# LSTM and a three-layer sign network: Wx's transfers in another order, two fewer steps of x Wx ahead of the recurrence

## The chip, the cores and the metric

The kernel runs on one core of one Trainium2 chip. The metric is the device time of that core in microseconds, the median of the runs shown. The profile is one further execution, taken by the hardware profiler; its own time stands beside its span below.

## The reference

An LSTM runs over 64 steps for 32 sequences, its hidden states go through three dense layers whose weights are +1 or −1, and the result is added to x.

```python
# x: (32, 64, 256), cond_1024: (32, 256) is h0, Wx and Wh: (256, 1024), b: (1024,)
xW = jnp.einsum('ntd,dg->ntg', x, Wx) + b
def step(carry, xw_t):
    prev_h, prev_c = carry
    a = xw_t + prev_h @ Wh
    i = jax.nn.sigmoid(a[:, :Hd])
    f = jax.nn.sigmoid(a[:, Hd:2 * Hd])
    o = jax.nn.sigmoid(a[:, 2 * Hd:3 * Hd])
    g = jnp.tanh(a[:, 3 * Hd:])
    next_c = f * prev_c + i * g
    next_h = o * jnp.tanh(next_c)
    return ((next_h, next_c), next_h)

# k0: (512, 1024), k1: (1024, 1024), k2: (1024, 256), booleans: True is 1, False is -1
h = jnp.concatenate([hs, -hs], axis=-1)
h = s0 * dense(k0, h)
h = jax.nn.relu(h) * 2
h = s1 * dense(k1, h)
h = jax.nn.relu(h) * 2
h = s2 * dense(k2, h)
return x + h
```

## The kernel before

**Layout.** 256 hidden units are four quarters (q) of 64. A time step's gates lie on 128 partitions, a quarter's 32 sequences on each 32 of them, and four gates of 64 columns side by side. A product for a time step is therefore cut into four column strips of TensorE (4 × 32), for two halves k of the contraction. Gates stand in slots in the order 3, 0, 1, 2 (`GATES`), so slots 1, 2 and 3 are neighbours in Wx as well. In the trace an fp32 product is two instructions.

**Before the loop.** VectorE clears `warm` and `idle`; TensorE runs two products of zeros into the gate banks and eight (`WARM_UP`) into `p_idle` (L643 to L646), while x's first eight steps and Wx come in over two DMA queues, that of SyncE (SP) and that of ScalarE (ACT). `load_gates` (L121) issues one transfer for a group of slots and a range of k; given two engines it cuts the 128 rows into halves. Loads on these two queues take turns on eight semaphores, so that a ninth load is issued after the landing of an earlier one. VectorE turns x (`turn_x`, L229), and TensorE forms x Wx for the first eight steps in four PSUM banks: k = 0 for slots 1 and 2, then k = 0 for slots 0 and 3, then `copy_bias` (L657; 16 small products and a copy by VectorE), then k = 1 for all slots, with an eviction by VectorE that adds the bias (`evict_x`, L261) after every second step. `x_products` (L275) then goes on up to time step `AHEAD`.

**The loop over 64 steps.** Each step has the gates' products from h (`gates_from_h`, L304), then `cell_step` (L322): sigmoid and tanh on ScalarE, products on VectorE, tanh(c), h, a transposition of h into `hist`, and two ScalarE copies of the next step's x part into the gate banks (L319, L320). TensorE fills the time of that chain with other work, in passes that a generator yields:

```python
goal = (t + 1) * total_x // X_STEPS if t < X_STEPS else (t + 1 - X_STEPS) * total_ffn // (T - X_STEPS)
while done < goal:
    left_over[0] = goal - done
    done += next(work)
```

In the first `X_STEPS` steps the passes are x Wx of the time steps from `AHEAD` on, four to a time step (L249; a pass is four products with two slots, or half of four with four slots). In the others they are the FFN of the blocks 0 to 2 of 16 time steps each (`ffn_block`, L588). Block 3 follows after the loop in `last_block`, another algorithm.

**The FFN's passes.** A block has 192 passes of one 128 × 512 product each: 32 in the first layer (L594), 128 in the second (L620), 32 in the third (L607). An accumulation that ends is taken by `evict` (L365): ScalarE's relu makes a high part (L368), VectorE the low part (L369), and the next layer multiplies both. The third layer goes along two accumulations behind the second; at the end of a block, after the second layer's last accumulation m = 7, the order is:

```python
yield from layer2([(0, last - 2), (0, last - 1), (1, last - 2)])
yield from layer2([(0, last), (1, last - 1), (1, last)])
outputs.append(output(b, po))
```

Each pair is two passes, one for the high and one for the low part. `output` is then taken step by step (VectorE's transpositions, the addition of x, the stores). The order on every engine is the order in which the program emits instructions: a step's evictions stand behind its `cell_step`. Conversions of the weights' bits (`make_w0`, `make_w1`, `make_w2`), splits of h into two parts (`split_h`) and sums for the last block are dealt out at the ends of steps.

Of the kernel before, what the change touches and what calls it, by code (L numbers as in the profile page):

```python
# [43 lines left out]
def lstm_ffn(ctx: ExitStack, tc: tile.TileContext, x, cond, wx_d, wh_d, b_d, k0_d, k1_d, k2_d, s0_d, s1_d, s2_d, out):  # L44
    nc = tc.nc
    P = 128
# [10 lines left out]
    TB = SB * N  # L57
# [1 line left out]

    GATES = (3, 0, 1, 2)  # L60

    AHEAD = 12
    X_STEPS = 21

    FIRST_CHORE = 2
    W2_STEP = 24
# [4 lines left out]
    const = ctx.enter_context(tc.tile_pool(name="const", bufs=1))  # L71
# [12 lines left out]
    def act(shape, dtype, name):  # L84
        return apool.tile(shape, dtype, tag="act", name=name)
# [5 lines left out]
    def load_x(i, half, engines, part=slice(0, SB // 2)):  # L91
        if part.start == 0:
            xq[i, half] = xpool.tile([P, SB // 2, HQ], F32, tag="x", name=f"x{i}_{half}")
        t0 = i * SB + half * (SB // 2)
        for q in range(NQ):
            engines[q % len(engines)].dma_start(  # L96
                out=xq[i, half][q * N : (q + 1) * N, part],
                in_=x[:, t0 + part.start : t0 + part.stop, ts(q, HQ)],
            )
# [5 lines left out]
    wx = wpool.tile([P, 2, G], F32, tag="wx", name="wx")  # L105
# [2 lines left out]
    w2 = const.tile([P, 2, FC1, P], F32R, name="w2")  # L108

    warm = const.tile([P, 40], F32, name="warm")  # L110
    nc.vector.memset(warm, 0.0)
    idle = const.tile([P, 512], mybir.dt.bfloat16, name="idle")
    nc.vector.memset(idle, 0.0)

    first = warm[:, 4 : 4 + N]
    nc.vector.memset(first[:1], 1.0)
# [4 lines left out]
    def load_gates(t, w_d, slots, engines, chunks=slice(0, 2)):  # L121

        w_rows = w_d.rearrange("(p b) g -> p b g", b=2)
        s0, n, g0 = slots[0], len(slots), GATES[slots[0]]
        if len(engines) == 1:
            halves = [slice(0, P)]
        else:
            halves = [slice(0, P // 2), slice(P // 2, P)]
        for engine, half in zip(engines, halves):
            engine.dma_start(  # L130
                out=t[half, chunks, s0 * H : (s0 + n) * H], in_=w_rows[half, chunks, g0 * H : (g0 + n) * H]
            )


    both = [nc.sync, nc.scalar]
    load_x(0, 0, both)
    for k in range(2):
        load_gates(wx, wx_d, (1, 2), [nc.sync], slice(k, k + 1))
        for slot in (0, 3):
            load_gates(wx, wx_d, (slot,), [nc.scalar], slice(k, k + 1))  # L140
    load_x(0, 1, both)
    load_gates(wh, wh_d, (1, 2), both)
    load_gates(wh, wh_d, (0,), [nc.scalar])
# [19 lines left out]
    for i in range(2):  # L163
        t = act([P, 2, F0], U8, f"k0_{i}")
# [64 lines left out]
    def turn_x(i, half, part=slice(0, SB // 2)):  # L229
        if part.start == 0:  # L230
            xT[i, half] = act([P, SB // 2, 2, N], F32, f"xT{i}_{half}")
        nc.vector.transpose(  # L232
            xT[i, half][:, part], xq[i, half][:, part].rearrange("p t (j b) -> p t b j", b=2)
        )
# [10 lines left out]
    def x_part(p, t, k, slots, start):  # L245

        i, s = divmod(t, SB // 2)
        for q in range(NQ):
            nc.tensor.matmul(  # L249
                p[q * N : (q + 1) * N, t % 2, slots],  # L250
                xT[i // 2, i % 2][:, s, k, :],
                wx_q[:, k, q, slots],
                start=start,
                stop=False,
                skip_group_check=True,
            )
# [4 lines left out]
    def evict_x(p, t):  # L261
        xg[t] = gpool.tile([P, 2, 4 * HQ], F32, tag="xg", name=f"xg{t}")
        b = bias.rearrange("p g j -> p (g j)").unsqueeze(1).to_broadcast([P, 2, 4 * HQ])
        load[0] += 1
        nc.vector.tensor_tensor(xg[t], p.rearrange("p t g j -> p t (g j)"), b, ALU.add)  # L265

    def next_x(half):

        if half < 2 * NB:
            load[0] += 1  # L270
            turn_x(*divmod(half, 2))
            if half + 4 < 2 * NB:
                load_x(*divmod(half + 4, 2), [nc.sync])

    def x_products(t0, t1):  # L275

        for t in range(t0, t1, 2):
            p = x_bank(t)
            for s in range(2):
                for k in range(2):  # L280
                    start = s == 0 and k == 0
                    passes = min(left_over[0], 2)
                    if passes == 1:
                        x_part(p, t + s, k, slice(0, 2), start)
                        yield 1
                        x_part(p, t + s, k, slice(2, 4), False)
                    else:
                        x_part(p, t + s, k, slice(0, 4), start)
                    if s == 1 and k == 1:
                        evict_x(p, t)  # L290
                        half, left = divmod(t + 2, SB // 2)
                        if left == 2 and half + 1 < 2 * NB:
                            turns.append(half + 1)
                        if left == 6 and turns:
                            next_x(turns.popleft())
                    yield passes
# [50 lines left out]
    def split_h(i):  # L347

        b, s = divmod(i, SB // SH)
        if s == 0:  # L350
            hparts[b] = (
                hpool.tile([P, 2, TB], F32R, tag="hhi", name=f"hhi{b}"),
                hpool.tile([P, 2, TB], F32R, tag="hlo", name=f"hlo{b}"),
            )
        hi, lo = (p[:, :, ts(s, SH * N)] for p in hparts[b])
        full = hist.pop(i)
        if b == NB - 1:

            hi, lo = (a.rearrange("p k (n t) -> p k t n", n=N) for a in (hi, lo))
            full = full.rearrange("p k (t n) -> p k t n", n=N)  # L360
        nc.scalar.copy(hi, full)
        nc.vector.tensor_tensor(lo, full, hi, ALU.subtract)
# [277 lines left out]
    outputs = deque()  # L640

    p_idle = ps_f.tile([P, TB], F32, tag="pf", name="p_idle")
    for g in gate_banks:  # L643
        nc.tensor.matmul(g, idle[:, :P], idle, start=True, stop=True)
    for n in range(WARM_UP):
        nc.tensor.matmul(p_idle, idle[:, :P], idle, start=True, stop=True)  # L646
    turn_x(0, 0, slice(0, SB // 4))
    turn_x(0, 0, slice(SB // 4, SB // 2))
    for i in range(4):
# [7 lines left out]
    def copy_bias():  # L657
        p_bias = ps_o.tile([P, 4, HQ], F32, tag="po", name="p_bias")
        for q in range(NQ):
            for i, t in enumerate(b_row):  # L660
                nc.tensor.matmul(  # L661
                    p_bias[q * N : (q + 1) * N, 2 * i : 2 * i + 2],
                    first,
                    t.rearrange("p g (q j) -> p q g j", q=NQ)[:, q],
                    start=(i == 0),
                    stop=True,
                    skip_group_check=True,
                )
        nc.vector.tensor_copy(bias, p_bias)

    banks = [x_bank(t) for t in range(0, SB // 2, 2)]
    for slots in (slice(1, 3), slice(0, 4, 3)):
        for t in range(SB // 2):
            x_part(banks[t // 2], t, 0, slots, t % 2 == 0 and slots.start == 1)
    copy_bias()
    for t in range(SB // 2):
        x_part(banks[t // 2], t, 1, slice(0, 4), False)
        if t % 2:
            evict_x(banks[t // 2], t - 1)
            if t == 1:  # L680
                turn_x(0, 1)
    nc.vector.transpose(hT, h_first.rearrange("p (j b) -> p b j", b=2))
    for _ in x_products(SB // 2, AHEAD):
        pass
# [3 lines left out]
    def ffn():  # L688
        for b in range(NB - 1):
            yield from ffn_block(b)  # L690
        yield from last_block(NB - 1)
# [8 lines left out]

    work = x_products(AHEAD, T)
    total_x = (T - AHEAD) * 4
    total_ffn = (NB - 1) * (4 * FC0 + 2 * FC0 * FC1 + 4 * FC1)
    done = 0
    for t in range(T):
# [5 lines left out]
        if outputs:  # L711
            load[0] += 1
            if next(outputs[0], "end") == "end":
                outputs.popleft()
        if t == X_STEPS:
            work, done = ffn(), 0
# [4 lines that stand above are left out]
        if t == X_STEPS - 1:  # L721
            next(work, None)

        if turns and load[0] < 2:
            next_x(turns.popleft())
        if splits and (load[0] < 2 or t >= X_STEPS or t == SH * splits[0] + 2 * SH - 1):
            split_h(splits.popleft())
        else:
# [4 lines left out]
            elif t >= W2_STEP and chores2:  # L733
                chores2.popleft()()
            if w0_parts and (load[0] < 2 or t == X_STEPS - 1):
                w0_parts.popleft()()
# [34 lines left out]
```

## Time and profile before

| | |
|---|---|
| median of 3 runs | 312.17 us (311.9 to 312.34) |
| profiled execution | 312.77 us, span 311.0 us |
| TensorE busy | 304.9 us, 98% |
| VectorE, ScalarE busy | 177.6 us, 143.1 us |
| first gates / first FFN step / last step | 17.4 / 80.8 / 260.0 us |
| moved by DMA | 10.88 MB |

In the rows of the profile PE is TensorE's products, PEld its weight loads, DVE is VectorE, ACT ScalarE, SP SyncE; L249 is line 249 of the kernel. A row of a timeline gives start, duration, engine, line, operation, out<-in, and in brackets the idle time before it and what ended it. Products are pipelined: a row's duration reaches beyond the start of the next, and the time that a product costs is read from start to start. A row of waits gives the total, the number of times and the longest. The span runs from the first instruction to the last; the profiled execution's time has 1.8 us around it.

### The profile page before, as it was taken

What the parts mean: (1) busy time and instruction counts of PE and PEld (TensorE: products, weight loads), DVE (VectorE), ACT (ScalarE), POOL (GpSimd) and SP (SyncE); (2) the same over time, 40 slices, a digit from 0 to 9 for tenths busy, and PEclk for the clock granted to TensorE, in tenths of its full rate; (3) what the DMA queues carried; (4) which work ended last, traced back from release to release, by engine and by line L of the source; (5) the groups of instructions that cost most, each with busy time, mean ns of one, the idle gap of its engine ahead of it and who ended that gap; (6) DMA issues with size and microseconds to landing.
All of it is one profiled execution on the core that took longest, in us unless ns stands there. A gap on an engine that the chain in (4) does not pass through costs nothing.

```text
span 311.0 us, 9795 instructions
## 1 busy us (share of the span) xinstructions
PE 304.9 (98%) x4138; PEld 242.4 (78%) x4138; DVE 177.6 (57%) x527; ACT 143.1 (46%) x512; POOL 6.6 (2%) x24
## 2 busy tenths in 40 slices
PE   7999999999999999999999999999999999999994
PEld 3888888787777777777777777777777777899994
DVE  2466767777673444455755444568564444599441
ACT  0224657774564543444633433356443333786320
POOL 5300000000000000000000000000000000000000
PEclk9999999999999999999999999999999999999999
DMA  6864001143000000000010000000410000031001
GB/s 186 210 185 108 6 10 49 36 93 67 3 2 0 2 2 0 3 2 0 2 38 14 22 1 2 2 2 6 98 34 2 3 0 2 25 80 32 2 0 68
DMA packets 27450, 10.88 MB, mean 35 GB/s; under 512 B 23560, under 2 KB 26632, under 8 KB 27408
## 3 DMA queue, kind: packets, MB, share of 16 engines
q1 hardware_dynamic: 24768, 8.66, 11.3%
q10 hardware_dynamic: 2400, 1.57, 1.8%
q8 instruction: 32, 0.52, 0.7%
q14 instruction: 10, 0.08, 0.1%
q0 software_dynamic: 240, 0.04, 0.1%
HBM read 8.16 MB, written 2.10 MB: 33 GB/s over the span
## 4 chain that ended last, share of the span: by engine, by line
PE 96%; DMA 1%; DVE 1%; SPq 0%; ACT 0%; issue 0%; ACTq 0%
PE p L620 30%; PE gates L308 20%; PE px L249 18%; PE p L594 8%; PE po L607 7%; PE gates L459 4%; PE r L459 2%; PE x L459 2%; PE po L564 2%; PE p L486 2%; DMA wx<-in_L_cond_Wx_dram 1%; SPq L96 0%; DVE a_7l L369 0%; DVE o L574 0%; PE p_bias L661 0%
## 5 line engine op out<-in xcount | busy, mean ns | idle before, releaser
L308 PEld LDWEIGHTS gates<-wh,hist 128*32 128x32 f32 x2016 | 54.6, 109 | 22.3 <-issue 13.4
L308 PE MATMUL gates<-wh,hist 128*32 128x192 f32 x2016 | 68.1, 275 | 0.0
L249 PE MATMUL px<-wx,xT 128*32 128x256 f32 (+1 forms) x1168 | 60.7, 355 | 0.4 <-DMA wx<-in_L_cond_Wx_dram 0.4
L325 ACT ACTIVATE sig<-gates 128x128 f32<-128x128 f32 x64 | 17.7, 277 | 79.8 <-PE gates L308 79.6
L249 PEld LDWEIGHTS px<-wx,xT 128*32 128x32 f32 x1168 | 42.2, 111 | 12.3 <-DVE xT L232 1.3
L329 DVE TENSOR_TENSOR kept<-sig,c 128x64 f32<-128x64 f32 x63 | 14.2, 225 | 49.1 <-ACT sig L325 48.8
L335 ACT ACTIVATE th<-c 128x64 f32<-128x64 f32 x64 | 16.4, 257 | 31.4 <-DVE c L333 31.4
L337 DVE TENSOR_TENSOR h<-sig,th 128x64 f32<-128x64 f32 x64 | 14.4, 225 | 20.7 <-ACT th L335 20.7
L265 DVE TENSOR_TENSOR xg<-px,bias 128x512 f32<-128x512 f32 x32 | 21.2, 670 | 2.8 <-PE px L249 2.3
L319 ACT COPY gates<-xg 128x192 f32<-128x192 f32 x64 | 20.0, 313 | 1.5 <-DVE xg L265 1.5
L594 PE MATMUL p<-hhi,w 128*128 128x512 f32 x48 | 19.3, 402 | 0.0
L594 PE MATMUL p<-hlo,w 128*128 128x512 f32 x48 | 19.1, 397 | 0.0
L342 DVE STREAM_TRANSPOSE hist<-h 128x64 f32<-128x64 f32 x64 | 15.7, 245 | 2.4
L333 DVE TENSOR_TENSOR c<-kept,new 128x64 f32<-128x64 f32 x64 | 14.4, 225 | 2.2
L327 ACT ACTIVATE sig<-gates 128x64 f32<-128x64 f32 x64 | 14.9, 233 | 0.1
L326 ACT ACTIVATE cand<-gates 128x64 f32<-128x64 f32 x64 | 14.0, 218 | 0.0
L331 DVE TENSOR_TENSOR new<-sig,cand 128x64 f32<-128x64 f32 x64 | 13.9, 217 | 0.0
L320 ACT COPY gates<-xg 128x64 f32<-128x64 f32 x64 | 13.0, 203 | 0.0
L594 PEld LDWEIGHTS p<-hhi,w 128*128 128x128 f32 x48 | 9.0, 188 | 2.1
L594 PEld LDWEIGHTS p<-hlo,w 128*128 128x128 f32 x48 | 9.0, 188 | 1.9
L214 ACT ACTIVATE w<-bits,nsgn,sgn 128x1024 fp32r<-128x1024 uint8 x8 | 9.9, 1240 | 0.0
L620 PE MATMUL p<-a_7h,w 128*128 128x512 f32 x24 | 9.9, 412 | 0.0
(250 smaller groups left out, 603.1 us busy)
## 6 DMA issues: line engine op xcount, KB each, us to landing
x<-in_x_dram SPq DMA_DIRECT2D x52, 64.0 KB, 2.7
out_dram<-o SPq DMA_DIRECT2D x28, 64.0 KB, 1.8
bits<-in_L_ffn_k_dram SPq DMA_DIRECT2D x10, 128.0 KB, 2.7
wx<-in_L_cond_Wx_dram SPq DMA_DIRECT2D x2, 256.0 KB, 4.8
wx<-in_L_cond_Wx_dram ACTq DMA_DIRECT2D x4, 128.0 KB, 5.1
wh<-in_L_cond_Wh_dram ACTq DMA_DIRECT2D x2, 256.0 KB, 5.3
wh<-in_L_cond_Wh_dram SPq DMA_DIRECT2D x2, 256.0 KB, 5.8
k<-in_L_ffn_k_dram SPq DMA_DIRECT2D x2, 256.0 KB, 3.1
```

What stands on the lines that cost most here:

```text
L249: nc.tensor.matmul(p[q * N : (q + 1) * N, t % 2, slots], xT[i // 2, i % 2][:, s, k, :], wx_q[:, k, q, slots], start=start, stop=False, ski ...
L265: nc.vector.tensor_tensor(xg[t], p.rearrange("p t g j -> p t (g j)"), b, ALU.add)
L308: nc.tensor.matmul(g[q * N : (q + 1) * N], hT[:, k, :], wh_q[:, k, q, slots], start=False, stop=(k == 1), skip_group_check=True,)
L319: nc.scalar.copy(gates[0], x_t[:, :3])
L325: nc.scalar.activation(sig[:, 0:2, :], gates[0][:, 1:3], AF.Sigmoid)
L327: nc.scalar.activation(sig[:, 2, :], gates[1][:, 0], AF.Sigmoid)
L335: nc.scalar.activation(th, c, AF.Tanh)
L342: nc.vector.transpose(hT, h.rearrange("p (j b) -> p b j", b=2))
L459: nc.tensor.matmul(bank[pair][:, i], a(k)[:, ts(2 * pair + i, P)], b(k, n), start=first and i == 0 and k == 0 and n == 0, stop=last and k ...
L594: nc.tensor.matmul(p, w0[:, k, ts(m, P)], a[:, k, :], start=(n == 0), stop=(n == 3))
L607: nc.tensor.matmul(po[m], w2[:, m, k], a1[k][n], start=(k == 0 and n == 0), stop=(k == FC1 - 1 and n == 1))
L620: nc.tensor.matmul(p1[m], w1[:, k, ts(m, P)], a0[k][n], start=(k == 0 and n == 0), stop=(k == FC0 - 1 and n == 1),)
```

## The change

`AHEAD` goes from 12 to 10 and `X_STEPS` from 21 to 22, so 54 time steps of x Wx are dealt over 22 steps of the loop in place of 52 over 21, and the FFN's 576 passes over 42 in place of 43. `idle` shrinks from 512 columns to 128, is cleared ahead of `warm`, and is read four times over as the moving operand of the same ten zero products. Wx's six transfers become: slots 1 and 2 of k = 0 by halves of the rows on both queues, slot 3 on SP, slot 0 on ACT, then slots 1 to 3 of k = 1 on SP as one piece of 384 KB, and slot 0 of k = 1 on ACT. `copy_bias` moves from ahead of k = 1 to behind its second time step.

```diff
-    AHEAD = 12
-    X_STEPS = 21
+    AHEAD = 10
+    X_STEPS = 22
...
     warm = const.tile([P, 40], F32, name="warm")
+    idle = const.tile([P, P], mybir.dt.bfloat16, name="idle")
+    nc.vector.memset(idle, 0.0)
     nc.vector.memset(warm, 0.0)
-    idle = const.tile([P, 512], mybir.dt.bfloat16, name="idle")
-    nc.vector.memset(idle, 0.0)
...
     load_x(0, 0, both)
-    for k in range(2):
-        load_gates(wx, wx_d, (1, 2), [nc.sync], slice(k, k + 1))
-        for slot in (0, 3):
-            load_gates(wx, wx_d, (slot,), [nc.scalar], slice(k, k + 1))
+    load_gates(wx, wx_d, (1, 2), both, slice(0, 1))
+    load_gates(wx, wx_d, (3,), [nc.sync], slice(0, 1))
+    load_gates(wx, wx_d, (0,), [nc.scalar], slice(0, 1))
+    load_gates(wx, wx_d, (1, 2, 3), [nc.sync], slice(1, 2))
+    load_gates(wx, wx_d, (0,), [nc.scalar], slice(1, 2))
     load_x(0, 1, both)
...
     p_idle = ps_f.tile([P, TB], F32, tag="pf", name="p_idle")
+    zeros = idle.unsqueeze(1).to_broadcast([P, TB // P, P])
     for g in gate_banks:
-        nc.tensor.matmul(g, idle[:, :P], idle, start=True, stop=True)
+        nc.tensor.matmul(g, idle, zeros, start=True, stop=True)
     for n in range(WARM_UP):
-        nc.tensor.matmul(p_idle, idle[:, :P], idle, start=True, stop=True)
+        nc.tensor.matmul(p_idle, idle, zeros, start=True, stop=True)
...
-    copy_bias()
     for t in range(SB // 2):
         x_part(banks[t // 2], t, 1, slice(0, 4), False)
+        if t == 1:
+            copy_bias()
         if t % 2:
             evict_x(banks[t // 2], t - 1)
```

## The prediction

> **What bounds the kernel now.** I read the page first (busy shares, chain), then the timeline of TensorE at the start, at step boundaries of both halves of the loop and at the last step, then who waited for whom.
>
> The page:
>
> ```profile
> span 311.0 us, 9795 instructions
> PE 304.9 (98%) x4138; PEld 242.4 (78%) x4138; DVE 177.6 (57%) x527; ACT 143.1 (46%) x512; POOL 6.6 (2%) x24
> PE 96%; DMA 1%; DVE 1%; SPq 0%; ACT 0%; issue 0%; ACTq 0%
> ```
>
> TensorE is nearly always busy and is 96% of the chain that ended last. So the change can only matter where TensorE idles, switches or waits, and in how often it does so. The start, in the timeline of TensorE:
>
> ```profile
> 1.24 1.04 PE L644 MATMUL gates<-idle 128*128 128x512 bf16 x2 [1.24 <-DVE idle L113]
> 6.11 4.16 PE L249 MATMUL px<-wx,xT 128*32 128x128 f32 x128 [0.42 <-DMA wx<-in_L_cond_Wx_dram]
> 17.42 1.08 PE L308 MATMUL gates<-wh,hT_first 128*32 128x192 f32 x31
> ```
>
> After the zero products there is one hole, 0.42 us, put down to Wx; from 6.11 us on there is none before the first step at 17.42. Step boundaries, two stretches of the same view:
>
> ```profile
> 44.59 1.08 PE L308 MATMUL gates<-wh,hist 128*32 128x192 f32 x32
> 47.63 1.08 PE L308 MATMUL gates<-wh,hist 128*32 128x192 f32 x32
> 50.51 1.08 PE L308 MATMUL gates<-wh,hist 128*32 128x192 f32 x32
> 80.82 1.08 PE L308 MATMUL gates<-wh,hist 128*32 128x192 f32 x32
> 85.01 1.08 PE L308 MATMUL gates<-wh,hist 128*32 128x192 f32 x32
> 89.19 1.08 PE L308 MATMUL gates<-wh,hist 128*32 128x192 f32 x32
> ```
>
> A step with ten passes of x Wx takes 3.04 us (47.63 − 44.59), one with nine 2.88. A step with thirteen FFN passes takes 4.18. Who waited, TensorE's loads:
>
> ```profile
> PEld gates L308 <- issue: 13.4, 38, 0.4
> PEld po L607 <- DVE a_7l L369: 0.5, 1, 0.5
> ```
>
> The first row is the switch from FFN weights back to gate weights, about 0.35 us at 38 of the 43 FFN steps. The second is a real wait, once, in the last step, in the timeline:
>
> ```profile
> 260.01 1.08 PE L308 MATMUL gates<-wh,hist 128*32 128x192 f32 x32
> 262.74 0.40 PE L607 MATMUL po<-a_5l,w 128*128 128x512 f32 x1
> 262.98 0.40 PE L607 MATMUL po<-a_7h,w 128*128 128x512 f32 x1
> 263.49 0.50 PE L607 MATMUL po<-a_7l,w 128*128 128x512 f32 x1
> 263.82 0.39 PE L607 MATMUL po<-a_6h,w 128*128 128x512 f32 x1
> ```
>
> Undisturbed passes start 0.23 apart; here a_7h to a_6h takes 0.84 in place of 0.46, so 0.39 us are lost with more digits of the trace. This row decides my forecast.
>
> **The change, part by part.** Durations are those of the profiled execution: 312.77 us, span 311.0, so 1.8 outside the span. The three runs have a median of 312.17; I add differences to that.
>
> *Ten steps ahead in place of twelve.* Two time steps leave the stretch before the loop: 2 × 4 = 8 passes of 0.216 us (a step with ten passes has 2.16 us of them): −1.73.
>
> *Twenty-two x steps.* Before: (64 − 12) × 4 = 208 passes in 21 steps, 19 of ten and 2 of nine: 19 × 3.034 + 2 × 2.880 = 63.4, which is 80.82 − 17.42. After: 216 passes in 22 steps; (t + 1) × 216 // 22 gives nine at t = 0, 5, 11, 16 and ten in 18: 18 × 3.034 + 4 × 2.880 = 66.1. +2.73. A nine-pass step costs 2.88 and not 3.034 − 0.216 = 2.82, since there the recurrence ends last (the transposed h ends 0.15 us before the next gates, against 0.30 in steps of ten). VectorE must then not be late: in a nine-pass step an xg eviction (0.69) and a transposition of x (0.70) queued behind it end just where the next step's kept begins, as at 20.89 + 0.69 and 21.58 in step 0 now. The new nines have no more than that behind them, so 2.88 holds.
>
> *Forty-two FFN steps.* 576 passes stay 576. What goes is one step's fixed part: 4.18 − 13 × 0.227 = 1.23 us (gates 0.87, and 0.36 for the two switches). −1.23. The three edits together: −1.73 + 2.73 − 1.23 = −0.23: the step moved to the x half saves its switch, less twice 0.06 for the new nine-pass steps.
>
> *Where the FFN steps now end.* A block has 192 passes. 576 / 42 is 192 / 14, so every block now takes exactly 14 steps, and (k × 576) // 42 ends the thirteenth step at pass 178. Passes 179 and 180 end the last accumulation of layer 1 (m = 7); ScalarE must take relu of it (L368), VectorE the low part (L369); six passes of layer 2 follow, then pass 187 needs a_7h and 188 a_7l. All that falls into one step, with no gates between. Now, with 43 steps, block 0 stops at 174 and 187, with the gates between a_7h and a_7l, and block 1 at 169 and 183, with the gates three passes after m = 7: no wait in either (each such step is 4.18 or 4.41). Block 2 stops at 178: the one wait shown. After the change blocks 0 and 1 get it too, at t = 35 and 49. Its size there is read from an ordinary step with an eviction that is ready early, t = 47, which began at 191.78:
>
> ```profile
> 194.28 0.59 ACT L368 ACTIVATE a_6h<-p 128x512 fp32r<-128x512 f32 x1
> 194.90 0.69 DVE L369 SCALAR_TENSOR_TENSOR a_6l<-p,a_6h 128x512 fp32r<-128x512 f32 x1 [0.38 <-ACT a_6h L368]
> ```
>
> The relu starts 2.50 us into the step, since ScalarE is strictly behind its recurrence work and the two copies of the next step's x part (0.31 and 0.20); the low part ends at 194.90 + 0.69 − 191.78 = 3.81. In the last step there is no next step: the relu starts at 2.11, the low part ends at 3.42, and 0.39 are lost. 3.81 is 0.39 later, so 0.39 + 0.39 = 0.78 per block. Who waits behind: TensorE's remaining four passes of the block and all after them; the next gates have over 1.4 us of slack and hide none of it. Two blocks: +1.56. From both sides: at least 2 × 0.39, if the copies were out of the way; at most 2 × 1.1, were VectorE also turning an output of 0.41 us (outputs are over by then). I take 0.78.
>
> *Wx's order.* Six issues stay six (SP 2 to 3, ACT 4 to 3). What is needed first (slots 1 and 2, k = 0) is cut in two halves of 128 KB. Now SP's 256 KB piece, issued at 1.65, lands 4.32 later, at 5.97. But x's last quarter lands only at 5.2; VectorE starts to turn at 5.42, the first turn ends at 5.87, and TensorE's first load is at 6.08. So at most about 0.15 us is there to win. [...] By the row it is 0 to 0.15. [...] I take −0.10. The 384 KB piece and the rest of k = 1 are needed only at 10.3, and all of Wx now lands by 8.7: nothing.
>
> *Smaller memset.* VectorE's 0.27 becomes about 0.1, and it goes ahead of warm: the zero products start about 0.26 earlier, end at 5.2, and wait longer for x. Ten products of the same width stay. Directly 0. Through the clock: the zero products start 0.43 apart, a later pass of the same 512 columns 0.23, though the granted clock shows 1.00 throughout; the first x Wx products run at half rate until about 6.95. [...] By the row, moving it by 0.26 would gain 0.13; [...] I take 0.
>
> *Bias after t = 1.* The 16 products (0.47) stay. VectorE's copy moves from 10.8 to about 11.6, so its four evictions and the turn of the first h, which end at 15.07 now, end at about 15.4. The first gates will ask for that h at 15.6 (17.42 − 1.73 − 0.10), where they ask at 17.4 now: some 0.1 to spare after the 0.15 that a hand-over takes. Cost 0; some tenths if that cover is gone.
>
> *Wh.* Its last piece, ACT's, issued at 8.72, lands 6.7 later, at 15.4; the first gates ask at 15.6. The margin is 0.2, where it was 2. SP's and ACT's issues of Wh (7.4 to 8.7) wait for landings of Wx, which come in another order now; with the small pieces landing sooner Wh may be issued some tenths sooner, and behind the 384 KB piece as much later. I take 0, range 0 to +0.8. x of later blocks, k0 and the bits behind it on SP are needed after 20 us, and their issues don't move by more.
>
> Sum: −0.23 + 1.56 − 0.10 = +1.23: span 311.0 to 312.2, profiled time 312.77 to 314.0, median 312.17 to 313.4.
>
> **The rivals.**
> *A: no wait at a_7 (10%).* At t = 35 and 49 the pair is ready in time, so TensorE goes straight on. It decides from a low part that ends before about 3.2 us into the step in place of 3.81. For it: the row shows the wait once only. Against: VectorE and ScalarE run in order, and 3.81 recurs in the other steps. Time: 312.17 − 0.33 = 311.8, no slower.
> *B: Wh is late for the first step (18%).* The 0.2 us of margin are used up, and TensorE stands before its first gates. It decides from a landing after 15.6, and each us late is a us. At 0.8: 314.2.
> *C: the start gives more (5%).* x is held up less with smaller pieces behind it, landing near 4.2 like its third quarter, but only until Wx; −0.7 in place of −0.1: 312.8.
> That Wx's order does nothing for the time at all is inside my own case: 313.5.
>
> **How the numbers follow.** My case has 67%, 313.4, by itself 312.9 to 313.9. The range takes in C below and most of B above: 312.6 to 314.2; A is left out. About 0.2%, or 0.62 us, is what a measurement can tell from no change. Faster by that (under 311.55): 4%, from A with luck. Within: 12%, the rest of A and the low end of C. Slower: 84%.
>
> **What would show it.** Right: a wait PEld po on DVE a_7l of three times and about 2 us; steps t = 35 and 49 of 5.2 us; first gates near 15.6; 22 x steps, four of 2.88; FFN switches one fewer. Wrong: periods of 4.41 at 35 and 49 (then A); an idle TensorE before the first gates on DMA wh (B); x Wx starting before 5.6 (C).

## The result, and the profile after

The changed kernel takes 315.31 us (median of 6, 314.05 to 315.71) against 312.12 in the same session: ratio 1.0088, 95% interval 1.0074 to 1.0101. Forecast were 313.4 us in a range of 312.6 to 314.2. The direction was right, the size was not. Two of the six executions took 314.05 and 314.27 us, the other four 315.04 to 315.71. The profiled one is the shortest of the six; that matters below.

The page after:

```profile
span 312.1 us, 9797 instructions
PE 305.5 (98%) x4138; PEld 241.6 (77%) x4138; DVE 178.2 (57%) x527; ACT 143.4 (46%) x512; POOL 6.6 (2%) x24
PE 94%; DVE 2%; DMA 1%; ACT 1%; ACTq 0%; issue 0%
```

VectorE and ScalarE have a larger share of the chain that ended last, 2% and 1% where they had 1% and 0%. Who waited, TensorE's loads (total, times, longest; "issue" means that the engine waited for nothing that the profile shows):

```profile
PEld gates L309 <- issue: 12.5, 35, 0.5
PEld po L608 <- DVE a_7l L370: 1.6, 3, 0.5
PEld po L608 <- ACT a_7h L369: 0.9, 2, 0.4
```

The wait on a_7l comes three times, and a_7h is waited for as well. The step t = 35, timeline of TensorE and then of the two engines that it waits for:

```profile
138.14 1.08 PE L309 MATMUL gates<-wh,hist 128*32 128x192 f32 x32
...
140.87 0.39 PE L608 MATMUL po<-a_5l,w 128*128 128x512 f32 x1
141.29 0.49 PE L608 MATMUL po<-a_7h,w 128*128 128x512 f32 x1
142.01 0.50 PE L608 MATMUL po<-a_7l,w 128*128 128x512 f32 x1 [0.23 <-DVE a_7l L370]
142.35 0.40 PE L608 MATMUL po<-a_6h,w 128*128 128x512 f32 x1
...
143.37 0.53 PE L309 MATMUL gates<-wh,hist 128*32 128x192 f32 x8
```

```profile
140.64 0.59 ACT L369 ACTIVATE a_7h<-p 128x512 fp32r<-128x512 f32 x1
```

```profile
141.27 0.69 DVE L370 SCALAR_TENSOR_TENSOR a_7l<-p,a_7h 128x512 fp32r<-128x512 f32 x1 [0.38 <-ACT a_7h L369]
```

The step takes 5.23 us (143.37 − 138.14) in place of 4.41. The relu starts 2.50 into it and the low part ends at 3.82, both as forecast. So the loop did what the prediction said. The start, in TensorE's timeline:

```profile
0.99 1.04 PE L646 MATMUL gates<-idle 128*128 128x512 bf16 x2 [0.99 <-DVE warm L113]
6.27 4.56 PE L250 MATMUL px<-wx,xT 128*32 128x128 f32 x144 [0.86 <-DMA wx<-in_L_cond_Wx_dram]
15.64 1.08 PE L309 MATMUL gates<-wh,hT_first 128*32 128x192 f32 x32
```

x Wx starts later than before (6.27 against 6.11), though its first piece was put first, and the hole ahead of it has doubled (0.86 against 0.42): the zero products begin 0.25 earlier (0.99 against 1.24) and end as much earlier, and x Wx begins 0.16 later. VectorE starts to turn x at 4.29 here, 1.1 earlier than before: x is no longer what comes last, Wx is.

### The profile page after: what moved, and what is told of

Same layout as the page of the kernel before. It is cut to its first block, busy times and chain, and to the rows that moved or that the text cites. A ratio compares the mean times of both kernels' runs of the same rounds, so it can differ in the third digit from the quotient of the medians.

```text
span 312.1 us, 9797 instructions
## 1 busy us (share of the span) xinstructions
PE 305.5 (98%) x4138; PEld 241.6 (77%) x4138; DVE 178.2 (57%) x527; ACT 143.4 (46%) x512; POOL 6.6 (2%) x24
## 4 chain that ended last, share of the span: by engine, by line
PE 94%; DVE 2%; DMA 1%; ACT 1%; ACTq 0%; issue 0%
PE p L621 29%; PE gates L309 20%; PE px L250 18%; PE p L595 8%; PE po L608 6%; PE gates L460 4%; PE r L460 2%; PE x L460 2%; PE po L565 2%; PE p L487 2%; DMA wx<-in_L_cond_Wx_dram 1%; DVE a_7l L370 1%; ACT a_7h L369 0%; ACTq L96 0%; ACT sig L326 0%
## 5 line engine op out<-in xcount | busy, mean ns | idle before, releaser
L309 PEld LDWEIGHTS gates<-wh,hist 128*32 128x32 f32 x2016 | 54.6, 109 | 22.3 <-issue 12.0
L338 DVE TENSOR_TENSOR h<-sig,th 128x64 f32<-128x64 f32 x64 | 14.4, 225 | 20.7 <-ACT th L336 20.7
L334 DVE TENSOR_TENSOR c<-kept,new 128x64 f32<-128x64 f32 x64 | 14.4, 224 | 2.2
L621 PE MATMUL p<-a_0h,w 128*128 128x512 f32 x24 | 9.7, 405 | 0.0
```

Source lines behind the costliest of these rows:

```text
L309: nc.tensor.matmul(g[q * N : (q + 1) * N], hT[:, k, :], wh_q[:, k, q, slots], start=False, stop=(k == 1), skip_group_check=True,)
L621: nc.tensor.matmul(p1[m], w1[:, k, ts(m, P)], a0[k][n], start=(k == 0 and n == 0), stop=(k == FC0 - 1 and n == 1),)
```

## The experiments

The two profiled executions differ by 1.28 us, the medians by 3.19. So something differs between executions of one kernel, and I separated the parts first. Two theories run through the expectations: 'clock' holds that TensorE stays at half its rate for longer (fours of x Wx's products 0.213 us apart in e15, 0.109 in the short execution) when it has stood idle too long ahead of x Wx, 'Wh late' that the first gates wait for Wh. `before` and its median were taken anew beside each group: 312.35 for the first four runs, 312.43 for the second and third four, 312.45 for the last. Of the 147 executions of `before` in these groups three are long too: 313.82, 314.44 and 314.61.

**e1, the start alone.** The changed kernel with

```diff
-    AHEAD = 10
-    X_STEPS = 22
+    AHEAD = 12
+    X_STEPS = 21
```

> The changed start (Wx's order, small memset, bias later) with 12 steps ahead and 21 x steps as before. Theory 'clock': the zero products now end at 5.2 us and TensorE then stands for about 1 us, where it stood for 0.6; [...] Then single executions spread over 1.5 to 2 us, from about 311.8 to 313.8, and the median is 313.0 to 313.6. Rival 'Wh late': with 12 steps ahead the first gates come near 17.4 us, 2 us after Wh, so nothing is left to wait for; spread as before (0.6) and a median of 311.8 to 312.3.

Measured: 313.01 (22 runs), ratio 1.0023 (1.0011 to 1.0036). Sixteen executions lie between 312.23 and 313.55 and six between 314.01 and 314.20. The start costs by itself, and in two groups, as 'clock' has it; 'Wh late' alone can't make them with 12 steps ahead. The profile showed one thing that neither theory had: a second wait of 0.51 us for Wx in the middle of k = 0.

**e2, the loop alone.** The kernel before with

```diff
-    AHEAD = 12
-    X_STEPS = 21
+    AHEAD = 10
+    X_STEPS = 22
```

> The start of before with 10 steps ahead and 22 x steps. Both theories: steps t = 35 and 49 take 5.2 us (+0.81 each), less 0.23 for the moved step: +1.4, 313.5. Theory 'clock': executions lie within 0.6 as before's do, since the zero products end at 5.5 as before. Rival 'Wh late': the spread of 1.6 that the changed kernel shows is here, since the first gates come near 15.7 us with Wh landing at 15.4; median 314.5 to 315.

Measured: 313.89 (313.54 to 314.18), ratio 1.0051 (1.0039 to 1.0063). Steps 35 and 49 take 5.24 us each. Two times 0.84 less 0.23 is 1.45; the interval is 1.2 to 2.0. No second group. In its profile Wh landed at 14.9 and the first gates came at 15.14.

**e3, ten zero products in place of eight in p_idle.** The changed kernel with

```diff
-    WARM_UP = 8
+    WARM_UP = 10
```

> The changed kernel with two more zero products, so that the hole ahead of x Wx shrinks from 1.0 to about 0.2 us. Theory 'clock': the executions near 315.7 vanish, all lie between 313.6 and 314.5, median 314.0. Rivals 'Wh late' and 'Wx lands late in most executions': zero products change nothing of either, median near 315.3 and the spread of 1.6 stays.

Measured: 314.40 (314.31 to 314.91, 5 runs), nothing near 315.7. The median is 0.4 above what 'clock' expected. Its profile has the second wait for Wx too (0.41), and Wh landing as late as 16.2 with the first gates at 16.39: that part is 'Wh late'. Five runs are few for the absence of a group.

**e4, the block's end moved off the step's end.** The changed kernel with

```diff
-        goal = ... else (t + 1 - X_STEPS) * total_ffn // (T - X_STEPS)
+        goal = ... else (t + 1 - X_STEPS) * total_ffn // (T - X_STEPS) - 5 * (t < T - 1)
```

> The changed kernel with the goal of every FFN step but the last 5 passes lower, so that a block's last-but-one step ends at pass 173 and the gates stand between a_7h (187) and a_7l (188). Theory 'a_7': t = 35 and 49 fall from 5.22 to 4.41 and the wait of 0.39 in the last step goes as well: 2.0 less than the changed kernel, 313.3, with its spread of 1.6 kept; the wait PEld po on DVE a_7l is gone. Rival 'the 0.8 are not of a_7 but of the block's change': it stays at 315.3 and the long steps move.

Measured: 312.50 (312.03 to 313.55, 13 runs), ratio 1.0006 (0.9997 to 1.0015), 2.8 below the changed kernel's median in another session and 2.4 below e5's. Steps 35 and 49 fall to 4.41. Of the products none waits for a_7 any more, and of the third layer's loads one is left, in the last step, where there were five (three on a_7l, two on a_7h):

```profile
PE px L250 <- DMA wx<-in_L_cond_Wx_dram: 1.1, 1, 1.1
PE gates L646 <- DVE warm L113: 1.0, 1, 1.0
PEld po L608 <- DVE a_7l L370: 0.2, 1, 0.2
```

The three waits are 2.0 of that by the traces, and the shift takes them away: they come from where a block's end falls in the step. The median is 0.8 below the 313.3 that I expected. One of 13 executions (313.55) is near where a long one would lie (315.6 less 2.0), though the hole ahead of x Wx is as in the changed kernel; why so few were long is not known.

**e5, the changed kernel once more, without an edit.**

> The changed kernel once more, to see whether its times fall in two groups and to catch one of the long ones in a profile. Theory 'clock': spans of about 312.2 to 312.6 and, in a quarter or more of the executions, near 313.8; in a profile of a long one the first x Wx products start 0.213 apart by fours up to 9 us or later, where the short one has 0.107 from 6.3 on. Rival 'Wx or Wh lands late': in a long one the products keep 0.107 and TensorE stands for 1.5 us on a DMA.

Measured: 314.87 (6 runs), ratio 1.0091 (1.0069 to 1.0114). Four executions at 314.55 to 315.00, two at 315.95 and 316.93. The profile fell on one of the first group and tells nothing of the second.

**e6, a loop without the waits on the start of before.** The kernel before with e2's and e4's edits:

```diff
+    AHEAD = 10
+    X_STEPS = 22
...
+        goal = ... else (t + 1 - X_STEPS) * total_ffn // (T - X_STEPS) - 5 * (t < T - 1)
```

> The start of before, with 10 steps ahead, 22 x steps and goals 5 passes lower. Theory 'a_7': the loop's part without its two waits of 0.83 and without the one of 0.39 at the end: 313.9 of the loop alone less 2.05, about 311.85, or 0.4 to 0.5 below before (312.35), spread 0.6. Rival 'the waits move elsewhere': near 313.

Measured: 311.52 (311.40 to 312.24, 8 runs), ratio 0.9974 (0.9964 to 0.9984): faster than both kernels. The waits do not move elsewhere. What was to be had from 10 and 22 is there, once a block's end is not at a step's end.

**e7, two zero products fewer in the kernel before.**

```diff
-    WARM_UP = 8
+    WARM_UP = 6
```

> The kernel before with two zero products fewer: TensorE then stands from 4.6 to about 6.0 us, 1.4 in place of 0.6; no transfer is touched. Theory 'clock': some executions, a third to a half, come out 1.4 to 2.2 longer, near 314, and the others stay near 312.2. Rival 'DMA': the times stay as before's, 311.8 to 312.9.

Measured: 312.81 (14 runs), ratio 1.0020 (1.0004 to 1.0037). Seven executions lie at 312.05 to 312.60, seven at 313.01 to 314.55, while 22 of before in the same group end at 313.39. No transfer was touched, so the zero products alone can make long executions. But the profiled one, 313.01, had its full rate from the start and lost 0.85 us at 23.8 to something else:

```profile
24.66 1.93 PE L249 MATMUL px<-wx,xT 128*32 128x256 f32 x32 [0.47 <-issue]
```

TensorE waited there for nothing that the profile shows, some 0.5 us after a 16 KB packet on the instruction queue had landed, at 23.3. That is a second source of scatter, and not all of e7's spread is the clock's. That the packet is the cause is not shown: in e9, e12, e13 and e15 it lands as late (22.9 to 23.4), with TensorE further behind in its work, and nothing stands.

**e8, the changed kernel with Wx's transfers as before.**

```diff
-    load_gates(wx, wx_d, (1, 2), both, slice(0, 1))
...
+    for k in range(2):
+        load_gates(wx, wx_d, (1, 2), [nc.sync], slice(k, k + 1))
+        for slot in (0, 3):
+            load_gates(wx, wx_d, (slot,), [nc.scalar], slice(k, k + 1))
```

> The changed kernel with Wx's six transfers as before. Theory 'the new order lands what is needed first no earlier, and makes the hole longer': x Wx starts at 5.7 to 6.1 in place of 6.15 to 6.4, TensorE stands for 0.5 to 0.9, the long executions (near 315.6) are rare or gone, median 313.7 to 314.2. Rival 'memset and bias make the long ones': as the changed kernel, median near 315.3.

Measured: 314.51 (313.60 to 315.10, 6 runs), ratio 1.0064 (1.0048 to 1.0081). The median is 0.3 above the range that I gave and 0.8 below the rival's. x Wx started at 5.96, as expected. The profiled execution (315.07) lost 0.4 on Wh before the first gates and 0.62 in step 1, again at "issue", after a late instruction packet:

```profile
15.78 1.08 PE L308 MATMUL gates<-wh,hT_first 128*32 128x192 f32 x32 [0.31 <-DMA x<-in_x_dram]
20.07 0.26 PE L308 MATMUL gates<-wh,hist 128*32 128x64 f32 x4 [0.44 <-issue]
```

The first row names x, but Wh's last piece landed at 15.58 in the trace and it is Wh that the gates read: where a row's name doesn't fit, look at what else landed. Inconclusive on the long executions, with six runs.

**e9, six zero products fewer: what a late clock costs.** The kernel before with

```diff
-    WARM_UP = 8
+    WARM_UP = 2
```

> The kernel before with six zero products fewer: the zero products end at about 2.9 us, TensorE stands for 3 us before x Wx, no transfer is touched. Theory 'a late clock': [...] first starts 0.213 apart by fours, first gates 1.2 to 1.7 later; median 313.4 to 314.0. Rival 'the products of zeros don't matter for the time of what follows': 312.4 as before.

Measured: 314.02 (313.21 to 314.65), ratio 1.0050 (1.0037 to 1.0063). The profiled execution is the shortest:

```profile
5.51 5.13 PE L249 MATMUL px<-wx,xT 128*32 128x128 f32 x128 [2.38 <-DMA wx<-in_L_cond_Wx_dram]
17.79 1.08 PE L308 MATMUL gates<-wh,hT_first 128*32 128x192 f32 x31
```

Its 128 products of k = 0 take 5.13 us where e2 had 3.97, and the trace's clock record goes to full only at 8.50. It started 0.6 us earlier than the profiled execution of before and reached the first gates 0.4 us later.

**e10, e11 and e12, the start's three parts one by one, each in the kernel before.** The small memset:

```diff
     warm = const.tile([P, 40], F32, name="warm")
+    idle = const.tile([P, P], mybir.dt.bfloat16, name="idle")
+    nc.vector.memset(idle, 0.0)
     nc.vector.memset(warm, 0.0)
-    idle = const.tile([P, 512], mybir.dt.bfloat16, name="idle")
-    nc.vector.memset(idle, 0.0)
...
+    zeros = idle.unsqueeze(1).to_broadcast([P, TB // P, P])
```

> The kernel before with the small memset alone (zero products start 0.26 earlier and end 0.26 earlier). Theory 'clock': the hole is 0.5 to 0.9 in place of 0.3 to 0.6, still mostly harmless: 312.2 to 312.6, with an execution near 314 now and then. Rival 'the small memset makes the long executions': a third of them near 314, as the changed start has.

Measured: 312.40 (22 runs), ratio 1.0008 (0.9993 to 1.0022). Eighteen executions at 311.87 to 312.79, four at 314.14 to 314.44: no cost in the median, and four long ones in 22 where `before` has two in 55 in the same group.

The bias behind t = 1:

```diff
-    copy_bias()
     for t in range(SB // 2):
         x_part(banks[t // 2], t, 1, slice(0, 4), False)
+        if t == 1:
+            copy_bias()
```

> The kernel before with copy_bias moved behind t = 1 and nothing else. With 12 steps ahead nobody waits for VectorE's later evictions: 312.4, spread as before. Rival 'the moved products shift TensorE's instruction fetch', whose second load comes at 16 to 17.6 us in every profile with the moved bias and at 13.8 to 15.0 in those without: it comes after 16 here too, with a stand of 0.2 to 0.7 put down to issue in some executions, median 312.5 to 312.9.

Measured: 311.95 (17 runs), ratio 0.9988 (0.9981 to 0.9995). A gain of 0.2 to 0.6 that I had not expected; the second instruction packet came at 14.1 (15.0 in before), so the rival is wrong here (e1, also with 12 steps ahead but with Wx's new order, had it at 16.0). Where the gain comes from is not known.

Wx's order:

```diff
-    for k in range(2):
...
+    load_gates(wx, wx_d, (1, 2), both, slice(0, 1))
+    load_gates(wx, wx_d, (3,), [nc.sync], slice(0, 1))
+    load_gates(wx, wx_d, (0,), [nc.scalar], slice(0, 1))
+    load_gates(wx, wx_d, (1, 2, 3), [nc.sync], slice(1, 2))
+    load_gates(wx, wx_d, (0,), [nc.scalar], slice(1, 2))
```

> The kernel before with Wx's new order alone. Theory 'the order hurts': the first piece lands no earlier (x Wx starts at 6.0 to 6.4 where it can start at 5.6 to 6.1), slot 0 of k = 0 lands after 8.3 and TensorE stands 0.3 to 0.5 for it whenever the clock is up early; +0.3 to +0.6, 312.7 to 313.0, and some near 314. Rival 'the order is neutral': 312.4.

Measured: 313.53 (22 runs), ratio 1.0039 (1.0027 to 1.0052). Eight executions at 314.40 to 314.90, the others from 312.19 to 313.80. This is the part of the start that costs. TensorE's timeline of the profiled one (313.22):

```profile
2.07 3.29 PE L647 MATMUL p_idle<-idle 128*128 128x512 bf16 x8
6.33 1.96 PE L250 MATMUL px<-wx,xT 128*32 128x128 f32 x64 [0.98 <-DMA wx<-in_L_cond_Wx_dram]
8.73 1.96 PE L250 MATMUL px<-wx,xT 128*32 128x128 f32 x64 [0.45 <-DMA wx<-in_L_cond_Wx_dram]
```

Two losses can be read. The first piece is there no earlier: both halves must land, and ACT's landed at 6.24 (6.00 to 6.29 in the nine profiles with the new order). x Wx starts at 6.09 to 6.38 in the eight of them with eight or ten zero products in p_idle, and at 5.51 to 6.11 in the nine with the old order. And slot 0 of k = 0, now issued behind a half of the first piece, landed at 8.69; the 64 products that need only slots 1 and 2 are through by 8.3 when the clock is up, so TensorE stands 0.45 for it.

**e13, Wx's order alone with the hole closed.** e12 with

```diff
-    WARM_UP = 8
+    WARM_UP = 12
```

> Wx's new order alone, with four more zero products, so that TensorE has no hole before x Wx unless the clock is already up. Theory 'late clock': the executions at 314.4 and above (8 of 22 without them) vanish; what is left is the later start and the wait for slot 0, 312.4 to 313.8, median about 313.0. Rival 'the transfers themselves land late in those': 8 of 22 stay, median 313.5 or more.

Measured: 313.06 (22 runs, 312.51 to 313.78), ratio 1.0019 (1.0012 to 1.0026). All executions from 314.4 on are gone, 8 of 22 against 0 of 22, and no transfer was touched. TensorE's timeline:

```profile
2.06 4.89 PE L647 MATMUL p_idle<-idle 128*128 128x512 bf16 x12
6.88 3.34 PE L250 MATMUL px<-wx,xT 128*32 128x128 f32 x104
```

There is no idle time before 6.88. x Wx starts 0.55 later than in e12's profile (6.33), and the median is lower all the same. That settles the second group: it is made by the hole ahead of x Wx. Of e12's cost about half stays, +0.6, and that is the order's own.

**e14, e6 with the bias behind t = 1** (e6's edits and e11's).

```diff
+        if t == 1:
+            copy_bias()
```

> Wx's transfers and memset of before, 10 steps ahead, 22 x steps, goals 5 lower, and the bias behind t = 1 (which alone gave 0.4). If the parts add up: 311.5 less 0.4, about 311.1. Rival 'with 10 steps ahead the later evictions and the instruction fetch cost it back': 311.5 to 312.2.

Measured: 312.37 (311.69 to 314.14, 14 runs), ratio 0.9999 (0.9986 to 1.0012), where e6 had 0.9974 (0.9964 to 0.9984). The parts do not add up: with 10 steps ahead and these goals the later bias costs about 0.8 us, with 12 it gained 0.4 (e11). In the profile Wh landed at 15.69 and the first gates came at 15.89, and step 1 lost 0.35 at "issue", with the second instruction packet at 17.5, as in the profiles of e5 and e8. Of the eight profiles with the moved bias and 10 steps ahead seven have that packet at 16.3 to 17.6 (e3 at 15.5); e2 and e6, without the moved bias, have it at 13.8 and 14.4. So the packet is late as the rival has it. In the five of the eight whose step 1 is longer, by 0.15 to 0.62 us, it lands at 17.9 to 18.7, in the other three at 17.0 to 18.0. That fits, but the packet was not moved by itself; its part in the 0.8, and what delays it, stay open.

**e15 and e16, two single executions of the changed kernel, without an edit.**

> One look at the changed kernel, for a profile of a long execution (span near 313.8). Theory 'late clock': its first x Wx products start 0.213 apart by fours up to 9 us or more. Rival 'late transfers': they start 0.107 apart and TensorE stands 1.5 us for a DMA or for issue.

> A second look at the changed kernel, with the same expectations: in a long execution, products 0.213 apart by fours past 9 us by the theory of the late clock, 0.107 apart and a stand of 1.5 us for a DMA or for issue by that of late transfers.

Measured: 315.88 and 314.08. The first is a long one. TensorE's timeline:

```profile
1.82 3.62 PE L648 MATMUL p_idle<-idle 128*128 128x512 bf16 x8
6.37 6.51 PE L250 MATMUL px<-wx,xT 128*32 128x128 f32 x144 [0.93 <-DMA wx<-in_L_cond_Wx_dram]
17.45 1.09 PE L309 MATMUL gates<-wh,hT_first 128*32 128x192 f32 x31
```

The same 144 products take 6.51 us where the short execution of the changed kernel has 4.56. There is no other wait. How many were in work in a microsecond, those begun before it included, from the view of busy time in stretches (the number in brackets behind PE), first the long one, then the short:

```profile
7.20:8.20 1.00, 1.00 (x27) 1.00 (x22) 0.00 (x0) 0.00 (x0) 0.00 (x0) 1.00 0.71 174
8.20:9.20 1.00, 1.00 (x28) 1.00 (x24) 0.00 (x0) 0.00 (x0) 0.00 (x0) 1.00 0.56 126
```

```profile
7.20:8.20 1.00, 1.00 (x47) 1.00 (x40) 0.00 (x0) 0.00 (x0) 0.00 (x0) 1.00 0.72 178
8.20:9.20 1.00, 1.00 (x47) 1.00 (x40) 0.00 (x0) 0.00 (x0) 0.08 (x1) 1.00 0.51 116
```

27 or 28 against 47, with the column of the granted clock at 1.00 in both. By their start times in the trace 19 begin from 7.2 to 8.2 in the long one and 36 in the short, in fours 0.213 and 0.109 apart: half the rate. The first pieces of Wx landed alike (5.72 and 6.28 against 5.52 and 6.18). The trace's clock record goes to full at 10.42 us in the long one and at 5.26 in the short. First gates at 17.45 against 15.64, spans of 314.0 against 312.1: the 1.8 us of the start are the 1.9 us of the whole. The rival of late transfers is out for this execution.

## Why the prediction was wrong where it was

The terms of the sum, in us, the measured ones by the ratios and their intervals:

| term | forecast | measured |
|---|---|---|
| loop: 10 ahead, 22 steps, the waits at a_7 | +1.33 | +1.6 (1.2 to 2.0), e2 |
| Wx's order | −0.10 | +1.2 (0.8 to 1.6), e12; +0.6 (0.4 to 0.8) with the hole closed, e13 |
| smaller memset | 0 | +0.2 (−0.2 to 0.7), e10 |
| bias after t = 1 | 0 | −0.4 (−0.6 to −0.2) with 12 ahead, e11; +0.8 with 10, e14 against e6 |
| whole start | −0.10 | +0.7 (0.3 to 1.1) with 12 ahead, e1 |
| all | +1.23 | +2.7 (2.3 to 3.2); +2.8 (2.2 to 3.6), e5 |

**The loop: right.** "Steps t = 35 and 49 of 5.2 us" and "a wait PEld po on DVE a_7l of three times" are in the profile. 0.78 per block was taken, 0.82 to 0.84 measured (5.222 in the changed kernel and 5.243 in e2, less 4.407). The upper bound of 1.1 per block was a slip, 0.78 and 0.41 are 1.2; nothing rests on it. −0.23 for the moved step holds as well: four steps of 2.88, the others of 3.03, one FFN step fewer. The loop alone measured +1.5 (e2), forecast +1.33. Rival A has no place: the wait goes only if the block's end is moved (e4).

**The step that failed is "Wx's order … I take −0.10".** Measured alone: +1.1 in the medians (e12; 0.8 to 1.6 by the interval), about half of it through the clock, since +0.6 stays when the hole is closed (e13). The reason given, that x's landing bounds what there is to win, was read from one execution in which x came at 5.2. In the other profiles with the old order VectorE starts to turn x at 4.3 to 5.4; with the new order it starts at 4.1 to 4.5, and Wx's second half, at 6.00 to 6.29, is the last to land: cutting the piece in two made its landing the later of two queues'. The time was to be had from the trace of before (issues from 1.6 to 2.1, with KB and us from issue to landing):

```profile
wx<-in_L_cond_Wx_dram SPq DMA_DIRECT2D x1, 256.0 KB, 4.3
wx<-in_L_cond_Wx_dram ACTq DMA_DIRECT2D x1, 128.0 KB, 4.7
```

ACT's first piece of Wx, 128 KB issued at 1.69, landed at 6.40 there, 0.4 behind SP's 256 KB, and at 6.22 to 6.58 in all nine profiles with the old order. A half of 128 KB in its place lands at 6.00 to 6.29, hardly sooner. From 2.1 to 2.6 us both queues are at work in that trace, ACT's (q10) with 54.9% and SP's (q1) with 54.6% of the time of 16 engines. As an estimate from these two numbers, that left no time for a second queue to win. The −0.10 was an estimate of mine too, out of the 0 to 0.15 that the row of x gave, and no gain was measured. That slot 0 would land after its turn (8.6 to 8.7 in e1, e3 and e12, with 0.41 to 0.51 us of waiting) I had not priced.

**And "Through the clock … I take 0".** I looked at when the zero products begin and not at how long TensorE then stands. The traces' clock records and the rows of idle time, in us:

| profiled execution | idle ahead of x Wx | x Wx starts | record goes to full |
|---|---|---|---|
| changed kernel, short | 0.86 | 6.27 | 5.26 |
| `before` | 0.42 | 6.11 | 7.10 |
| e9 | 2.38 | 5.51 | 8.50 |
| changed kernel, long (e15) | 0.93 | 6.37 | 10.42 |

In the short execution the rate was full ahead of the 0.86 us of standing, and the products behind it start 0.109 apart by fours: it was not lost there. In e15 it was not yet full when TensorE stood, and became so 4.05 us after x Wx began. The price is half of the time that x Wx runs at half rate: 6.37 to 10.42 in e15, so 2.0; its products show 1.95. e13 shows it from the other side: without the hole none of 22 executions is long.

Long were 6 of 22 in e1, 2 of 6 in e5, 4 of 6 in the result, 8 of 22 in e12 and 7 of 14 (above 313) in e7, with 0.86 to 1.33 us of idle time in their profiles, and 3 of 147 of `before` with 0.42. The length of the hole is not all: e10, which has the small memset alone, has 4 of 22, and e4, with 1.05, at most one of 13. What decides in a single execution when the rate becomes full is not shown, so no share of long executions can be worked out ahead.

**The sum hid it.** I added differences to one profiled execution. That of before (312.77) had its clock at full only at 7.10 us, 0.99 after x Wx began, which costs about half of that, and lay 0.6 above its median; that of the changed kernel is the shortest of six. The two differ by 1.28, near my +1.23, and both facts are accidents of the start: that the forecast agrees with this pair is luck, and it missed the medians. Chance is in the medians too: with two long executions of six, as in e5, that of the changed kernel would have been lower.

**Rival B had part of it.** The margin of Wh is gone: in the profiles of the changed kernel Wh's last piece lands at 15.1 to 15.6 and TensorE is ready at about 15.4 in the profiled one, which waits 0.26 for it. I gave it 18% and a single size; it is there in some executions, beside the late instruction packet (0.15 to 0.6 us in step 1 of several). Loop (1.6) and start (0.7 by e1, with 12 steps ahead) make 2.3 of the 2.7 or 2.8 that the changed kernel measures. The rest would fit these two, which need 10 steps ahead to be felt, but it is no larger than the intervals. What is clear of them is the bias: "Cost 0; some tenths if that cover is gone" is +0.8 with 10 ahead (e14 against e6), and how that divides between Wh and the packet stays open. Rival C, an earlier x Wx, has the wrong sign: x did land near 4.1, and Wx did not follow.

## What to carry to other kernels

When work is dealt out evenly over steps, look where a stage's end falls within a step: here 576 passes over 42 steps put every block's last eviction into the same step as the product that needs it, and five passes of shift take 2.0 us of waiting away. A start is judged by all that must have landed, the later half of each cut piece included. Let a warm-up end too late rather than too early: reaching up to the first real product it left none of 22 executions long (e13), where 8 of 22 were (e12), and in e15 a hole of 0.93 us was followed by 4.05 us at half rate, which cost 1.95. And a forecast from one profiled execution should ask first how that execution stands to the median, and why.

## What of the hardware was not expected

- The granted clock reads 1.00 in every row while products start at half the pace (e15: fours 0.213 us apart against 0.109); only their spacing, or the clock's record in the trace, tells.
- Up to 0.85 us at about 19 to 24 us in which TensorE waits for nothing that the profile shows, soon after a 16 KB packet on the instruction queue landed late (e7, e8, e14); that the packet causes it is not shown. Such a packet takes 0.88 to 1.66 us in the profiles of `before` and of the changed kernel, with medians of 1.17 and 1.15.
- Two halves of 128 KB on two queues, issued at 1.66 and 1.70, landed at 5.0 to 5.8 and 6.00 to 6.29; one piece of 256 KB, issued at 1.65 on one queue, at 5.4 to 6.0.
